# A new written-out order for the attention part of a four-layer graph-network kernel

## The chip, the core and the metric

The kernel runs on one core of one Trainium2 chip. Five engines work beside each other, each through its own list of instructions in the order in which they stand: TensorE (PE in the profile; its weight loads are PEld), VectorE (DVE), ScalarE (ACT), GpSimd (POOL) and SyncE (SP), which in this part only issues DMAs. An instruction that waits holds up everything behind it on its engine. The metric is the device time in microseconds; the median of three runs is 1857.78 us (1857.74 to 1858.48).

## The reference, cut to what matters

The input `x` is 128 batches of 64 tokens with 256 features, float32. Four layers follow, each `x = x + f(relu(layernorm(x)))`: a graph convolution with batch norms, two convolutions with four LSTMs over windows of tokens, and two attentions. Only the attentions are touched by the change:

```python
# layer 2: one head, causal, the adjacency added to the scores
q, k, v = jnp.split(h @ Wqkv, 3, axis=-1)
scores = jnp.einsum('btd,bsd->bts', q, k) / 16 + adj       # lower triangle only
x = x + (softmax(scores) @ v) @ Wo
# layer 3: four heads of 64, masked where adj == 0
q, k, v = heads(h @ W)
x = x + softmax(q @ k.T / 8 + mask) @ v
```

Here `h` is `relu(layernorm(x))` of each layer.

## The kernel before

The 8192 rows of `x` are cut into 16 chunks of 512 rows (8 batches each). Until about 1483 us of the span the first two layers run; the change leaves them alone. The attention part then takes each chunk through some 45 named steps. No scheduler decides the order: `FIRST`, `ROUND` and `LAST` (from L2234) are three strings of words such as `score2+0` (step `score2` of chunk 0), and `run` (L2270) calls the steps as they stand, `FIRST` once, `ROUND` for c = 4 to 11 with numbers relative to c, `LAST` once. A step issues its instructions on each engine that it needs, so the order of the words is the order on every engine, SP's queue of DMAs included.

Steps of layer 2, for one chunk:

- `load2` gets the chunk's normalized rows, turned to channels, from DRAM (four DMAs of 128 KB, L268). For chunks 2 to 13 they were put there during the LSTMs; chunks 14 and 15 are normalized here (`norm2`, `apply2`, `chan2`).
- `q2`, `copyq2`, `v2a`, `v2b` project queries and values for the first chunks (L1526, L1519). From chunk 4 on, seven smaller products do it: `wz`, `w5`, `w6`, `w3`, `w7`, `w4` (L1773, L1776), with `sums2` on POOL for their operands and `w11`, `w12` adding on DVE.
- `score2` (L1836) multiplies queries with keys in 64x64 pieces, `exp2`, `divide2` and `turn2` (L1668, two transposes) make the softmax, `out2` (L1867) multiplies with the values and adds to `xs`.

Steps of layer 3: `norm3` (or `norm3a`, `norm3b`) and `apply3` normalize; `square3` transposes 32x32 squares on DVE (L286) and stores to DRAM, `load3` gets the rows back as channels; `sums_h` makes operands on POOL; `qa`, `q5`, `q6`, `q3`, `qc`, `qd` (L1938) and `va`, `v5`, `v6`, `v3`, `v7`, `v4` (L2062) project, with additions `c11`, `c12`, `v11`, `v12` on DVE; `score3` (L2025), `exp3`, `sum3`, `divide3`, `turn3` and `out3` (L2142) are the attention; `keep` stores `xs` to DRAM and `back` gets it in another row order as the tile `x`; `store` adds `x` to the result (L2157) and writes it out. For chunk 15 the last steps come in two halves (`score3h`, `exp3a`, `exp3b` and so on). `res1` (three calls for each of chunks 14 and 15: transposes and store, get, add) and `pair1` (store, get) finish the LSTM layer for the last two chunks. `sums_g`, `sums_v` and `sums_w` (words for combinations of weights) run once on POOL.

`score2`, `score3`, `out2` and `out3` use PE in narrow tiles (64 rows or columns, or 32); everything else uses it whole. PSUM has eight banks, taken by the pool in order of their release; the tiles `x` and `hT3` have two buffers, `td`, `td2` and `qk` one.

Of the kernel before, what the change touches and what calls it, by code (L numbers as in the profile page):

```python
# [19 lines left out]
def kernel(  # L20
# [1440 lines left out]
    def new_hT(sc):  # L1461

        hTs[sc] = l1r.tile([P, KD, SUP * CH], F32, tag="hT", name=f"hT_{sc}")
# [99 lines left out]
    RESIDUAL_LAST = (0, 4, 5.5), (3, 5, 9)  # L1563
    FIRST = (0.5, 0.5, 1, 3, 3, 4, 4, 5, 5.5, 7, 8, 9, 10, 10), (2, 3, 4, 5, 5, 5.5, 6, 9.5, 11, 11.5, 13, 14, 15, 15.5, 17, 18, 20)
    AHEAD = (9, 10), (10, 11)
# [31 lines left out]
    with tc.manual_schedule(engines={mybir.EngineType.PE, mybir.EngineType.DVE, mybir.EngineType.Pool,  # L1597
# [4 lines left out]
        for sc in range(last + 1):  # L1602
            todo = {}

            def units(places, unit):
                for n in places:
                    todo.setdefault(n, []).append(unit)


            if sc < last:  # L1610
                for i in range(SUP):
                    units((CONV if sc else FIRST)[i], convs[(sc + 1) * SUP + i])
                new_hT(sc + 1)
# [610 lines left out]
    def store(c, t):  # L2224
# [3 lines left out]
        for r in range(2):  # L2228
# [2 lines left out]

    FIRST = """score2+0 exp2+0 divide2+0 score2+1 v2a+1 v2b+1 load2+2 res1+15 res1+14 turn2+0 exp2+1  # L2234
               res1+15 divide2+1 load2+4 v2a+2 out2+0 q2+2 norm3+0 copyq2+2 turn2+1 apply3+0 load2+3 v2b+2
               out2+1 weights3+0 score2+2 res1+14 exp2+2 norm3+1 v2a+3 q2+3 divide2+2 chan3+0 apply3+1
               res1+14 v2b+3 square3+1 turn2+2 res1+15 v3a+0 v3b+0 change+0 out2+2 sums_g+0 sums2+4 load3+1
               q30+0 k30+0 sums_v+0 norm3+2 sums_h+1 copyq2+3 q31+0 k31+0 keep+0 score2+3 apply3+2 pair1+14
               score3+0 wz+4 w5+4 sums_w+0 v5+1 exp2+3 w11+4 qa+1 q5+1 c11+1 va+1 divide2+3 exp3+0 q6+1
               square3+2 q3+1 v6+1 turn2+3 c12+1 w6+4 load2+5 v7+1 sum3+0 back+0 v3+1 qc+1 divide3+0 w7+4  # L2240
               pair1+15 load3+2 w3+4 qd+1 v11+1 turn3+0 w4+4 v4+1 sums2+5 w12+4 score3+1 pair1+14 v12+1
               pair1+15"""
    ROUND = """out3-4 store-4 sums_h-2 exp3-3 out2-1 norm3a-1 norm3b-1 score2+0 sum3-3 wz+1 w5+1 qa-2 va-2
               w6+1 load2+2 q6-2 exp2+0 q5-2 w11+1 v5-2 divide3-3 v11-2 keep-3 back-3 apply3-1 c11-2 qc-2
               w7+1 v6-2 q3-2 divide2+0 w3+1 square3-1 w4+1 w12+1 qd-2 v7-2 sums2+2 c12-2 turn3-3 load3-1
               v3-2 v4-2 v12-2 turn2+0 score3-2"""
    LAST = """out3+8 keep+9 exp3+9 out2+11 score2+12 w5+13 keep+11 norm3a+11 store+8 sums_h+10 qa+10 sum3+9
              norm3b+11 divide3+9 wz+13 q6+10 c11+10 exp2+12 w11+13 va+10 turn3+9 apply3+11 keep+10
              divide2+12 q5+10 norm2+14 w6+13 v6+10 qc+10 square3+11 w3+13 turn2+12 v5+10 v7+10 out2+12
              apply2+14 w7+13 norm3a+12 q3+10 c12+10 qd+10 norm3b+12 v4+10 v11+10 w4+13 load3+11 chan2+14  # L2250
              out3+9 w12+13 sums_h+11 apply3+12 back+10 score3+10 back+9 score2+13 qa+11 v3+10 norm2+15
              q5+11 q6+11 square3+12 v12+10 c11+11 va+11 q3+11 keep+12 sums2+14 exp3+10 v6+11 qc+11 sum3+10
              v5+11 divide3+10 wz+14 c12+11 v7+11 exp2+13 qd+11 store+9 w6+14 w11+14 v4+11 divide2+13
              score3+11 w5+14 turn2+13 load3+12 w7+14 out2+13 v3+11 w4+14 turn3+10 w3+14 apply2+15
              norm3a+13 sums_h+12 w12+14 exp3+11 norm3b+13 qa+12 score2+14 apply3+13 v11+11 v12+11 out3+10
              chan2+15 store+10 square3+13 q6+12 exp2+14 v5+12 sums2+15 divide2+14 sum3+11 va+12 q5+12
              wz+15 v11+12 load3+13 v6+12 w11+15 turn2+14 qc+12 v7+12 divide3+11 v3+12 c11+12 back+12 q3+12
              c12+12 back+11 out2+14 v12+12 w6+15 qd+12 w5+15 norm3a+14 v4+12 w7+15 sums_h+13 norm3b+14
              score3+12 turn3+11 w3+15 w4+15 apply3+14 exp3+12 qa+13 w12+15 score2+15 out3+11 exp2+15
              square3+14 keep+13 q5+13 va+13 sum3+12 divide2+15 store+11 q6+13 v5+13 q3+13 turn2+15 c11+13  # L2260
              c12+13 qc+13 out2+15 norm3a+15 v6+13 v3+13 v7+13 norm3b+15 qd+13 v4+13 load3+14 apply3+15
              divide3+12 sums_h+14 score3+13 qa+14 turn3+12 square3+15 q5+14 c11+14 exp3+13 v11+13 q6+14
              out3+12 sum3+13 back+13 load3+15 va+14 v5+14 q3+14 qc+14 v6+14 store+12 c12+14 v3+14 qd+14
              v12+13 divide3+13 score3+14 v7+14 q30+15 keep+15 v12+14 exp3+14 back+15 k30+15 q31+15 sum3+14
              k31+15 turn3+13 divide3+14 keep+14 score3h+15 exp3a+15 out3+13 sum3a+15 exp3b+15 divide3a+15
              store+13 v3a+15 v3b+15 turn3a+15 turn3+14 back+14 v11+14 v4+14 sum3b+15 out3a+15 divide3b+15
              storea+15 turn3b+15 out3+14 out3b+15 store+14 storeb+15"""
    assert (NCH, SUP) == (16, 2)

    def run(order, c):  # L2270
        for name in order.split():
            i = max(name.find("+"), name.find("-"))
            steps[name[:i]](c + int(name[i:]))

    with tc.manual_schedule(engines={mybir.EngineType.PE, mybir.EngineType.DVE,
                                     mybir.EngineType.Activation, mybir.EngineType.Pool,
                                     mybir.EngineType.SP}):
        run(FIRST, 0)
        for c in range(4, 12):
            run(ROUND, c)  # L2280
        run(LAST, 0)
    close_l2()
# [49 lines left out]
```

## Time and profile before

| | us |
|---|---|
| median of three runs | 1857.78 (1857.74 to 1858.48) |
| profiled execution, its own time | 1858.88 |
| span of its trace, first to last instruction | 1857.1 |
| first PE instruction of the attention part (`score2+0`) | 1490.76 |
| PE busy over the span | 1816.6 (98%) |
| DVE, ACT, POOL busy | 1350.6, 1058.3, 653.3 |
| issue of the last store, `storeb+15` | 1853.17 |

The profiled execution's own time is 1.8 us above its span and 1.1 us above the median. An engine's row in the timeline gives the start, the duration and, in square brackets, how long the engine had idled and what ended that; `issue` there means that the engine waited for nothing that the profile shows. PEclk is the share of the full clock that PE was granted.

### The profile page before, as it was taken

To read this page: it belongs to the slowest core of one execution; us is meant where nothing else is said; L and a number is where in the kernel's file an instruction comes from. 1 tells how busy PE (TensorE), PEld (TensorE's weight loads), DVE (VectorE), ACT (ScalarE), POOL (GpSimd) and SP (SyncE) were. 2 spreads that over 40 slices of the span, in tenths; PEclk is the share of its full clock that TensorE was granted. 3 is DMA by queue.
4 is the path that set the end of the run, shared out by engine and by line. 5 is a ranking of instruction groups with operands and counts; after the bars stand their busy time and mean duration, and the time that the engine had idled before them with its cause. 6 is when DMAs were issued, how large, how long until landed. Compare 5 with 4: busy or idle time off the path is not lost.

```text
span 1857.1 us, 41626 instructions
## 1 busy us (share of the span) xinstructions
PE 1816.6 (98%) x15847; PEld 1532.7 (83%) x15847; DVE 1350.6 (73%) x3475; ACT 1058.3 (57%) x2538; POOL 653.3 (35%) x916
## 2 busy tenths in 40 slices
PE   8999999999999999999999999999999989999997
PEld 6877866996997898799699789789979868988885
DVE  5768857667677677777877776876667667888786
ACT  5766636556557466565665655746565644445453
POOL 5865713223214323322322322332132224444432
PEclk9999999999999999999999999999999999999999
DMA  3223652133443343242353444433244145454434
GB/s 116 70 61 138 233 207 64 62 114 125 148 126 125 114 160 125 90 150 83 123 160 115 148 131 142 148 113 126 82 137 131 45 126 165 148 160 151 138 116 137
DMA packets 113417, 234.56 MB, mean 126 GB/s; under 512 B 11713, under 2 KB 77121, under 8 KB 113217
## 3 DMA queue, kind: packets, MB, share of 16 engines
q1 hardware_dynamic: 112320, 230.02, 37.8%
q8 instruction: 126, 2.06, 0.5%
q0 software_dynamic: 320, 1.05, 0.2%
q10 hardware_dynamic: 576, 0.82, 0.1%
q14 instruction: 75, 0.61, 0.1%
HBM read 164.21 MB, written 67.63 MB: 125 GB/s over the span
## 4 chain that ended last, share of the span: by engine, by line
PE 86%; DVE 6%; ACT 2%; issue 2%; POOL 2%; DMA 1%; SPq 1%; DVEq 0%; POOLq 0%; ACTq 0%
PE x L1186 22%; PE z L1186 11%; PE y L1186 6%; PE y L1133 4%; PE x L1368 4%; PE y L1368 3%; PE u L948 3%; PE v L934 3%; PE x L1133 3%; PE X L1938 2%; PE X L436 2%; PE X L512 2%; PE z L1133 2%; PE v L2062 1%; PE Y L1938 1%
## 5 line engine op out<-in xcount | busy, mean ns | idle before, releaser
L1101 ACT ACTIVATE l_gates<-l_gates,bias 128x256 f32<-128x256 f32 (+4 forms) x528 | 238.1, 498 | 211.1 <-DVE l_gates L1195 109.8
L1186 PE MATMUL x<-xd,wset 128*128 128x128 f32 (+2 forms) x1152 | 254.9, 303 | 0.8 <-ACT l_gates L1192 0.8
L1186 PE MATMUL x<-l_hd,wset 128*128 128x128 f32 (+2 forms) x1152 | 254.5, 303 | 0.0
L1252 POOL TENSOR_TENSOR l_gates<-l_gates 128x512 f32<-128x512 f32 (+2 forms) x48 | 75.3, 1569 | 368.5 <-ACT l_gates L1101 368.5
L1186 PEld LDWEIGHTS x<-xd,wset 128*128 128x128 f32 x1152 | 187.7, 191 | 6.4 <-issue 1.4
L1195 DVE TENSOR_TENSOR l_gates<-l_gates,x 128x128 f32<-128x128 f32 (+2 forms) x384 | 121.3, 322 | 97.7 <-PE x L1186 95.1
L1186 PEld LDWEIGHTS x<-l_hd,wset 128*128 128x128 f32 x1152 | 187.8, 191 | 5.0
L1195 DVE TENSOR_TENSOR l_gates<-l_gates,z 128x128 f32<-128x128 f32 (+2 forms) x384 | 102.5, 319 | 104.8 <-PE z L1186 102.8
L1186 PE MATMUL z<-l_hs,wset 128*128 128x128 f32 (+2 forms) x768 | 147.1, 304 | 0.7 <-DVE l_hs L1110 0.7
L1186 PE MATMUL z<-hT,wset 128*128 128x128 f32 (+2 forms) x768 | 146.2, 303 | 0.0
L1192 ACT COPY l_gates<-y 128x128 f32<-128x128 f32 (+2 forms) x192 | 53.2, 290 | 137.6 <-PE y L1186 131.5
L1186 PEld LDWEIGHTS z<-l_hs,wset 128*128 128x128 f32 x768 | 116.8, 191 | 5.8 <-DVE l_hs L1110 2.5
L1186 PEld LDWEIGHTS z<-hT,wset 128*128 128x128 f32 x768 | 117.1, 191 | 3.3
L1101 ACT ACTIVATE l_gates<-x,bias 128x128 f32<-128x128 f32 (+2 forms) x216 | 84.9, 393 | 28.6 <-PE x L1186 25.9
L327 POOL TENSOR_TENSOR xd<-hT 128x128 f32<-128x128 f32 (+2 forms) x72 | 42.2, 586 | 127.6 <-DVE hT L1112 113.8
L1186 PE MATMUL x<-hT,wset 128*128 128x128 f32 (+2 forms) x384 | 85.8, 305 | 0.0
L1186 PE MATMUL x<-l_hs,wset 128*128 128x128 f32 (+2 forms) x384 | 84.9, 303 | 0.0
L1186 PE MATMUL y<-l_hd,wset 128*128 128x128 f32 (+2 forms) x384 | 83.2, 309 | 0.0
L1186 PE MATMUL y<-xd,wset 128*128 128x128 f32 (+2 forms) x384 | 81.6, 304 | 0.0
L1267 ACT ACTIVATE l_gates<-l_cell 128x256 f32<-128x256 f32 (+2 forms) x144 | 55.3, 384 | 45.8 <-DVE l_cell L1266 45.2
L328 POOL TENSOR_TENSOR xd<-hT 128x128 f32<-128x128 f32 (+3 forms) x80 | 51.4, 643 | 67.0 <-DVE hT L1116 29.5
L1110 DVE TENSOR_TENSOR l_hs<-l_gates 128x256 f32<-128x256 f32 (+4 forms) x120 | 51.4, 429 | 29.5 <-ACT l_gates L1159 13.8
(408 smaller groups left out, 4695.9 us busy)
## 6 DMA issues: line engine op xcount, KB each, us to landing
wset<-wfar SPq DMA_DIRECT2D x96, 896.0 KB, 8.4
hT<-far_h SPq DMA_DIRECT2D x124, 128.0 KB, 4.2
far_h<-hm SPq DMA_DIRECT2D x16, 512.0 KB, 3.0
far_n<-xs SPq DMA_DIRECT2D x16, 512.0 KB, 3.3
xs<-far_n SPq DMA_DIRECT2D x64, 128.0 KB, 2.8
far_x<-xs SPq DMA_DIRECT2D x16, 512.0 KB, 4.2
x<-far_x SPq DMA_DIRECT2D x64, 128.0 KB, 2.7
xt<-in_x_dram SPq DMA_DIRECT2D x15, 512.0 KB, 3.9
```

The costliest lines, as they stand in the source:

```text
L328: lambda: ((third or engine).tensor_tensor(t3, b22, b12, OP.subtract), engine.tensor_tensor(t2, b22, t1, OP.subtract)),
L934: nc.tensor.matmul(banks[m], wg0_sb[:, k, m * P : (m + 1) * P], agg[:, k, :], start=(k == 0), stop=(k == KD - 1))
L948: nc.tensor.matmul(banks[j // 2][:, j % 2, :], v[:, k, j * P : (j + 1) * P], wg1_sb[:, k, :], start=(k == 0), stop=(k == KD - 1))
L1101: nc.scalar.activation(gate(q, c, part), src, AF.Tanh if q == 2 else AF.Sigmoid, bias=bs[:, q * KD + c : q * KD + c + 1])
L1133: nc.tensor.matmul(folded(self.psum(kind)), wsets[p, self.q][:, BLOCKS[kind][0], :], ox[0][kind], start=kind in (1, 5), stop=True, skip_gr ...
L1186: nc.tensor.matmul(folded(self.psum(kind)), wsets[p, self.q][:, BLOCKS[kind][i], :], (ox[self.s] if part == "x" else oh)[kind], start=firs ...
L1192: nc.scalar.copy(gate(self.q, kind // 5, halves[kind // 5]), self.psum(kind))
L1195: nc.vector.tensor_add(gate(self.q, *dst), gate(self.q, *a), self.psum(kind))
L1252: nc.gpsimd.tensor_mul(gates[:, 0, :, :n], gates[:, 0, :, :n], gates[:, 2, :, :n])
L1267: nc.scalar.activation(gate(2, c, part), cells[:, c, part], AF.Tanh)
L1368: nc.tensor.matmul(folded(ps(g, kind)), single_block(KINDS1[kind])[:, g, :], right[kind], start=kind in (2, 5, 1), stop=True, skip_group_c ...
L1938: nc.tensor.matmul(st[c, tag][:, i * CH // 2 : (i + 1) * CH // 2].rearrange("p (a n) -> p a n", n=P), w, operand3(c, kind), start=first an ...
```

## The change

Only the three strings are written anew; no step is changed. The steps in each string, with the chunks that they are called for, move between the strings: the new `FIRST` also holds `out3+0`, `store+0` and `score2+4`, and `ROUND` begins with `w3+1` instead of `out3-4`. In `FIRST` the reloads of chunks 2 and 3 (`load2`) stand ahead of that of chunk 4 with one store of `res1` between each two. In `ROUND` `out2` stands alone among full-width products, and `score2`, `score3`, `out3` follow each other. In `LAST` the ways from a store to its reload change both ways: from `keep` to `back` there are now 126, 30 and 45 steps for chunks 13, 14 and 15 (36, 12 and 3 before) but 6 and 13 for chunks 11 and 12 (124 and 62 before); from `square3` to `load3` 16 and 15 for chunks 13 and 15 (11 and 9 before), and 7, 14 and 12 for 11, 12 and 14 (16, 26 and 22 before).

```diff
-    FIRST = """score2+0 exp2+0 divide2+0 score2+1 v2a+1 v2b+1 load2+2 res1+15 res1+14 turn2+0 exp2+1
-               res1+15 divide2+1 load2+4 v2a+2 out2+0 q2+2 norm3+0 copyq2+2 turn2+1 apply3+0 load2+3 v2b+2
-               out2+1 weights3+0 score2+2 res1+14 exp2+2 norm3+1 v2a+3 q2+3 divide2+2 chan3+0 apply3+1
...
+    FIRST = """v2a+1 score2+0 load2+2 exp2+0 score2+1 res1+14 v2b+1 q2+2 exp2+1 divide2+0 turn2+0 divide2+1
+               load2+3 copyq2+2 res1+15 load2+4 v2a+2 out2+0 turn2+1 res1+15 norm3+0 v2b+2 weights3+0
+               score2+2 out2+1 q2+3 apply3+0 exp2+2 v2a+3 norm3+1 res1+14 v2b+3 copyq2+3 divide2+2 chan3+0
+               apply3+1 turn2+2 res1+15 score2+3 res1+14 v3a+0 exp2+3 v3b+0 square3+1 change+0 out2+2
+               sums_g+0 q30+0 k30+0 q31+0 sums2+4 divide2+3 turn2+3 pair1+15 norm3+2 load3+1 k31+0 sums_h+1
+               apply3+2 out2+3 score3+0 sums_w+0 norm3a+3 wz+4 keep+0 qa+1 norm3b+3 w5+4 load2+5 w6+4 q6+1
+               w3+4 pair1+15 w11+4 square3+2 sums_v+0 w12+4 back+0 q5+1 exp3+0 w7+4 keep+1 va+1 q3+1 v11+1
+               c11+1 qc+1 wz+5 c12+1 v6+1 sum3+0 divide3+0 v5+1 qd+1 pair1+14 w4+4 turn3+0 apply3+3 v7+1
+               sums2+5 score2+4 score3+1 load3+2 out3+0 pair1+14 w6+5 exp2+4 store+0 keep+2 w5+5 divide2+4
+               v4+1 qa+2"""
-    ROUND = """out3-4 store-4 sums_h-2 exp3-3 out2-1 norm3a-1 norm3b-1 score2+0 sum3-3 wz+1 w5+1 qa-2 va-2
-               w6+1 load2+2 q6-2 exp2+0 q5-2 w11+1 v5-2 divide3-3 v11-2 keep-3 back-3 apply3-1 c11-2 qc-2
-               w7+1 v6-2 q3-2 divide2+0 w3+1 square3-1 w4+1 w12+1 qd-2 v7-2 sums2+2 c12-2 turn3-3 load3-1
-               v3-2 v4-2 v12-2 turn2+0 score3-2"""
+    ROUND = """w3+1 turn2+0 keep-1 square3-1 w7+1 exp3-3 va-2 v3-3 w4+1 sums_h-2 load2+2 q6-2 c11-2 q5-2
+               w11+1 sum3-3 v6-2 w12+1 v12-3 divide3-3 load3-1 qc-2 v5-2 v11-2 out2+0 v7-2 qd-2 sums2+2
+               back-3 norm3a+0 q3-2 norm3b+0 turn3-3 c12-2 v4-2 wz+2 apply3+0 score2+1 exp2+1 score3-2
+               out3-3 store-3 divide2+1 w6+2 w5+2 qa-1"""
-    LAST = """out3+8 keep+9 exp3+9 out2+11 score2+12 w5+13 keep+11 norm3a+11 store+8 sums_h+10 qa+10 sum3+9
...
-              out3+12 sum3+13 back+13 load3+15 va+14 v5+14 q3+14 qc+14 v6+14 store+12 c12+14 v3+14 qd+14
-              v12+13 divide3+13 score3+14 v7+14 q30+15 keep+15 v12+14 exp3+14 back+15 k30+15 q31+15 sum3+14
-              k31+15 turn3+13 divide3+14 keep+14 score3h+15 exp3a+15 out3+13 sum3a+15 exp3b+15 divide3a+15
-              store+13 v3a+15 v3b+15 turn3a+15 turn3+14 back+14 v11+14 v4+14 sum3b+15 out3a+15 divide3b+15
-              storea+15 turn3b+15 out3+14 out3b+15 store+14 storeb+15"""
+    LAST = """sums_h+10 va+10 turn2+12 square3+11 exp3+9 w11+13 back+9 v3+9 v11+10 w7+13 load3+11 sum3+9
...
+              v5+13 store+11 divide3+12 turn3+12 v6+13 square3+14 divide2+15 c11+13 v12+12 turn2+15 qc+13
+              out2+15 norm3a+15 norm3b+15 v7+13 out3+12 qd+13 load3+14 v3+13 v4+13 c12+13 sums_h+14
+              apply3+15 keep+15 score3+13 va+14 qa+14 square3+15 q5+14 store+12 v11+13 q6+14 v6+14 c11+14
+              q3+14 v5+14 c12+14 exp3+13 qc+14 sum3+13 qd+14 divide3+13 load3+15 score3+14 v12+13 keep+14
+              v7+14 exp3+14 v3+14 turn3+13 q30+15 v11+14 sum3+14 k30+15 q31+15 v12+14 divide3+14 k31+15
+              turn3+14 score3h+15 out3+13 exp3a+15 sum3a+15 v3a+15 back+13 v4+14 divide3a+15 exp3b+15
+              back+15 v3b+15 turn3a+15 out3+14 store+13 sum3b+15 divide3b+15 back+14 out3a+15 storea+15
+              turn3b+15 store+14 out3b+15 storeb+15"""
```

## The prediction, made before the changed kernel ran

> **What bounds the kernel now.** First the page: one engine has no slack over the span, and the chain that ended last lies on it.
>
> ```profile
> PE 1816.6 (98%) x15847; PEld 1532.7 (83%) x15847; DVE 1350.6 (73%) x3475; ACT 1058.3 (57%) x2538; POOL 653.3 (35%) x916
> q8 instruction: 126, 2.06, 0.5%
> PE 86%; DVE 6%; ACT 2%; issue 2%; POOL 2%; DMA 1%; SPq 1%; DVEq 0%; POOLq 0%; ACTq 0%
> ```
>
> The change adds no product and removes none, so only PE's idle time, its slow time and the tail after it can move. Next the busy time by stretch: FIRST, one period of ROUND, the end.
>
> ```profile
> core 0: us, PE busy (x) PEld busy (x) DVE busy (x) ACT busy (x) POOL busy (x), PEclk, DMA share, GB/s
> 1483.00:1560.00 77.00, 71.22 (x776) 54.72 (x775) 48.79 (x122) 32.07 (x69) 27.12 (x41) 0.96 0.47 129
> 1602.00:1622.70 20.70, 20.70 (x301) 18.78 (x301) 17.30 (x38) 10.40 (x21) 9.26 (x13) 1.00 0.51 154
> 1808.00:1827.60 19.60, 17.84 (x271) 14.16 (x273) 16.35 (x33) 8.70 (x18) 6.94 (x7) 1.00 0.41 122
> 1827.60:1857.10 29.50, 19.93 (x366) 14.13 (x356) 18.36 (x33) 7.84 (x14) 3.99 (x3) 0.92 0.46 154
> ```
>
> A period is full: PE 20.7 of 20.7 us. Idle time is in FIRST and at the end. PE's timeline shows the largest piece, then a second kind of gap:
>
> ```profile
> 1506.92 1.20 PE L1836 MATMUL s<-hT,qv 128*64 128x64 f32 x32
> 1512.92 3.75 PE L1519 MATMUL v<-wg_sb,hT 128*128 128x256 f32 x8 [4.80 <-DMA hT<-far_n]
> 1516.46 4.42 PE L1526 MATMUL p_q<-hT,wg_sb 128*128 128x512 f32 x8
> ...
> 1642.67 0.92 PE L1836 MATMUL s<-hT,qv 128*64 128x64 f32 x22 [0.60 <-issue]
> ...
> 1706.27 0.62 PE L1867 MATMUL o<-qv,att 64*32 64x256 f32 x4 [1.48 <-issue]
> ...
> 1753.48 0.63 PE L1836 MATMUL s<-hT,qv 128*64 128x64 f32 x8 [2.07 <-issue]
> ```
>
> The first: `v2a+3` waits for chunk 3's reload. SP's timeline says why it is late: that reload is issued last, behind two stores that wait for DVE's transposes until 1499.85, a get and chunk 4's reload.
>
> ```profile
> 1490.42 1.74 SPq L268 DMA_DIRECT2D hT<-far_n  x4
> 1499.85 2.31 SPq L261 DMA_DIRECT2D far_h<-hm  x2
> 1503.07 1.77 SPq L268 DMA_DIRECT2D hT<-far_h  x4
> 1504.94 3.70 SPq L268 DMA_DIRECT2D hT<-far_n  x8
> ```
>
> Its price is more than 4.80: `score2+2`'s slot lasted 6.00 us instead of 1.13, and `v` then took 3.54 instead of 1.73 and `p_q` 4.25 instead of 3.46 while PEclk was 0.66 (1510 to 1520). Together 7.5.
>
> The second kind waits for no engine and always stands inside a run of narrow tiles. The trace's packets on q8 are 16384 bytes each. Counting PE's records (weight load, product and separate wait one each, two loads and two products to a float32 product, one of each to a transpose), the four stalled records, with one more at 1579.89, are 24769, 26561, 28353 and 29633: each 193 above a multiple of 256. So PE takes its program in blocks of 256 records, and one came late: the records before took 2.3 to 3.0 us, and the block was there 3.6 to 4.7 us after its predecessor began. Slots lengthened by .60, .88, 2.09 and 2.46, the last with 1.55 of slow clock after it: 7.6.
>
> **What the Trainium skill says.** "Runtime: NRT & Kernel Launch", Instruction fetch mechanics: instructions come in blocks of 16 KiB (256 instructions), fetched over the engine's own DMA queue, and the cost is mostly hidden. The trace has the same block; hidden it is not, where 256 narrow records run in under 3 us. "TensorE: Matmul & The Clock Gate", Part 1: an idle window of about 3.4 us halves the clock. The trace agrees after 4.80 us of idling, and shows it after 2.07 too. "TensorEngine Tiling (Array Packing)", Key Properties: changing the tiling mode drains the engine. Here the last full-width step before a narrow run takes 0.31 instead of 0.22 and the first after it 0.54 instead of 0.43: 0.19 a run.
>
> **The change, part by part.** I divide the time at PE's first record of `score3h+15`. Before: from 1490.76 to 1837.87, 347.1 us. Steps at their undisturbed durations (`wz` 1.75, `q5` 0.87, `v5` 0.45, `score2` 1.13, `score3` 1.02, `out3` 1.04, `out2` 1.03, `turn3` 0.88 and so on) sum to 317.7; 26 narrow runs at 0.19 give 4.9; 24.5 remain. Of these 7.5 and 7.6 are named, and 9.4 are waits in FIRST (1.1) and LAST (8.3; the longest is 1.49 at `turn3+12`, behind DVE's `divide3+12`). From `score3h+15` to the end of the span are 19.2.
>
> Work: the same, but `turn3+14` now stands before `score3h+15` (+0.9): 318.6.
>
> Reloads: `load2+3` now follows one store of `res1`. DVE reaches those four transposes after both score masks, at about 1495.9, and takes 2.0; store at 1498.0, `load2+3` issued to 1500.1, landed by 1504.3 (4.1 from issue). `q2+3`, its first reader, has 16.8 us of PE work ahead of it: 1507.6. Cover 3.3 us. Queued behind on SP: `load2+4`, both gets, `w3`'s weights (1508.6, landing 6.5 later at 1515.1; `v3a+0` wants them at 1517.1). So -7.5. Next late in FIRST is `q6+1`: `sums_w` runs on POOL behind `score3+0`'s subtraction, which waits for DVE's maximum at about 1534.0; 1.9 plus two of 0.73 give 1537.5, PE is there at 1536.65: 0.9.
>
> Narrow runs: 40 instead of 29 in all, 37 instead of 26 before `score3h+15`: 37 x 0.19 = 7.0 (+2.1).
>
> Blocks: I numbered the new order's records the same way (nine more separate waits). Two boundaries 193 above 256k now have less than 3.6 us to the next inside narrow tiles: 28 records into `score2+5` (2.4 us to the next) and 60 into `score2+10` (2.1 us). By the four measured arrivals the stalls would be 1.2 to 2.3 and 1.5 to 2.6 if triggered as there; the first begins near full-width work, where fetches started up to 2.2 us before the boundary, so I take 0.8 and 1.7: 2.5 (range 0 to 5, and 1.5 more if the clock falls). A third block starts four records ahead of a run, with the fetch begun well before: 0.
>
> ROUND's waits: laid out from PE's `w3+1` as zero, every step's inputs are ready. The shortest slack is DVE's: `score3`'s product ends at 16.3, then masks 1.33, maximum 1.13, `store` 1.2, `divide2` 1.05: 21.1; `turn2` of the next period stands at 21.6. Then `w7`'s addition (2.8) before `w4` (3.4). Behind `turn2` all of PE waits, so 0.5 is all the cover. I take 0. On SP, `load3` waits for its store (2.9 landing) with `back` queued behind; `qa` needs the tile 9.5 us later, `store` the other 7.
>
> LAST, laid out the same way from the durations of before: `turn2+15` 0.5 (`divide2+15`); `v4+13` 0.9, because `v7+13`'s addition stands on DVE behind both `norm3+15` halves; `qd+14` 0.9 for `qc+14`'s addition, and `score3+14` 0.8 for ACT's copy of `qd+14`, as `qd+14` stands just before it; 0.2 elsewhere: 3.3. Gaps under 0.6 that such a layout misses (variations of copies and DVE slowed beside POOL) came to 3.3 in the trace of before; I add 2.0. The short way of chunk 11 from `keep` to `back` sits with `load3+13` behind it; the tile lands some 2 us before `qa+13`.
>
> The tail: `score3h`, DVE's halves, `store+13`, then `back+14` into the buffer that `store+13` frees, `store+14`, `storeb+15`. DVE's and SP's order in it is the same: 19.2.
>
> Sum: 1490.8 + 318.6 + 7.0 + (0.9 + 2.5 + 3.3 + 2.0) + 19.2 = 1844.3 span. The median before stands 0.7 above the span of the profiled execution (whose own time is 1.8 above): 1845 us.
>
> **Rivals.** *Half the gain* (1849 to 1854): both block stalls at their high end with slow clock (+4), LAST as costly as before (+3.0 over my 5.3). For it: all its steps moved and each of my waits is one reading of a chain; against it: the banks and buffers that LAST's steps take are free in my layout by 0.1 us or more.
>
> *The reload's wait moves* (1854.1 to 1861, within 0.2%): the change doesn't do what it says. If chunk 3's rows land 4 us later than worked out, PE stalls again at `q2+3` and its clock falls. For it: SP still has a waiting store ahead of the reload; against it: one with four transposes, not eight, and 3.3 us of cover.
>
> *DVE's half microsecond in ROUND* (1862 to 1870): if the chain from `score3` to `divide2` runs over by more than 0.5 us, each of eight periods loses what is over, before `turn2`: 8 us for each us. To end 0.2% above the kernel before takes 16.5 us more than the forecast, 2.1 a period, so an excess of 2.6 from which it decides. For it: this is the one chain without room. Against it: DVE is 17.3 of 20.7 us busy, and its operations lasted the same in every period before.
>
> **How the numbers follow.** The forecast (1840 to 1849) has 0.68, half the gain 0.20, the moved wait 0.07, DVE 0.05. From this faster by over 0.2% has 0.88, within 0.2% (about what a measurement here can tell from no change) 0.06, slower 0.06. The range must leave out no more than 2 in 10: 1840 to 1854 holds the first two.
>
> **What would show it.** PE's wait on `hT<-far_n` at L1519 or L1526 gone, and no PEclk near 0.66 near 1515. Two `issue` gaps, inside or after `score3`/`out3` near chunk 5 and chunk 10, together 1 to 5 us. Periods of ROUND of 20.95 us, 0.19 over the undisturbed ones before. `score3h` near 1825, and the end 19.2 later. Wrong would be: a repeated wait of `tr` L1668 on DVE in ROUND, waits of PE on DMA in LAST, or a tail longer than 20.

## The result, and the profile after

The changed kernel takes 1845.45 us (median of 4 runs, 1844.12 to 1846.00) against 1858.13 us for the kernel before, run beside it: a ratio of 0.993 with a 95% interval of 0.9913 to 0.9947. The prediction was 1845.0. Its profiled execution has a span of 1842.3 us (own time 1844.12) where the one before had 1857.1.

The page after, the parts that answer to those shown before: busy time of each engine, the queue of PE's program, and the chain that ended last.

```profile
PE 1812.8 (98%) x15847; PEld 1530.5 (83%) x15847; DVE 1353.4 (73%) x3475; ACT 1061.0 (58%) x2538; POOL 656.5 (36%) x916
q8 instruction: 125, 2.05, 0.5%
PE 88%; DVE 5%; ACT 2%; POOL 2%; DMA 1%; issue 1%; SPq 0%; ACTq 0%; DVEq 0%; POOLq 0%
```

The products are the same 15847. In the chain that ended last, `issue` (time in which an engine waited for nothing that the profile names) falls from 2% to 1%, and DVE's share from 6% to 5%. Where the time lay is in the busy time by stretch:

```profile
core 0: us, PE busy (x) PEld busy (x) DVE busy (x) ACT busy (x) POOL busy (x), PEclk, DMA share, GB/s
1483.00:1560.00 77.00, 76.11 (x826) 60.58 (x825) 56.99 (x143) 38.35 (x81) 33.44 (x48) 1.00 0.55 161
1510.00:1520.00 10.00, 10.00 (x77) 8.37 (x75) 7.63 (x19) 7.11 (x15) 3.37 (x5) 1.00 0.53 135
1602.00:1622.70 20.70, 20.70 (x300) 18.71 (x299) 17.20 (x38) 10.78 (x21) 9.61 (x12) 1.00 0.51 148
1808.00:1823.00 15.00, 13.63 (x117) 8.51 (x116) 11.17 (x17) 5.55 (x10) 1.90 (x1) 1.00 0.64 187
1823.00:1842.00 19.00, 10.01 (x288) 8.36 (x285) 10.56 (x22) 4.15 (x8) 2.09 (x2) 0.85 0.35 111
```

From 1483 to 1560 PE is busy for 76.11 us of 77 (71.22 before); from 1510 to 1520 it is full at full clock. SP's timeline shows the reload of chunk 3, the first row of `hT<-far_n` here, issued between the two stores (the second is chunk 4's):

```profile
1497.74 0.34 SPq L261 DMA_DIRECT2D far_h<-hm  x1
1498.13 2.23 SPq L268 DMA_DIRECT2D hT<-far_n  x4
1503.11 0.34 SPq L261 DMA_DIRECT2D far_h<-hm  x1
1503.55 2.24 SPq L268 DMA_DIRECT2D hT<-far_n  x4
```

What PE still waits for from 1483 us to its last work, all that the chain of waits lists:

```profile
PE X L1938 <- POOL ws L1745: 0.9, 1, 0.9
PE X L1938 <- DVE qk L1985: 0.9, 1, 0.9
PE o L2142 <- DVE att L2213: 0.8, 1, 0.8
PE o L2142 <- issue: 0.7, 1, 0.7
PE tr L2208 <- DVE s L1659: 0.7, 2, 0.5
PE v L2062 <- DVE v L2075: 0.6, 1, 0.6
PE p_q L1526 <- DMA hT<-far_h: 0.4, 1, 0.4
PE tc_n L240 <- DVE o L2157: 0.4, 1, 0.4
PE tr L1668 <- DVE s L1659: 0.2, 1, 0.2
```

Columns: total us, times, longest. Together 5.6 us; the same list of the kernel before adds up to 16.5, with 4.8 for the reload and 4.5 under `issue`. The first row is `q6+1` behind `sums_w`, the second `qd+14`, the sixth `v4+13`; the third and fifth lie in the tail, and the seventh is `q30+15`, which waits for chunk 15's rows. One late block is left, in PE's timeline:

```profile
1679.29 0.21 PE L2142 MATMUL o<-v,att 64*64 64x64 f32 x1 [0.66 <-issue]
```

### The profile page after: what moved, and what is told of

It reads as the page before. It is cut to its first block, busy times and chain, and to the rows that moved or that the text cites. A ratio compares the mean times of both kernels' runs of the same rounds, so it can differ in the third digit from the quotient of the medians.

```text
span 1842.3 us, 41656 instructions
## 1 busy us (share of the span) xinstructions
PE 1812.8 (98%) x15847; PEld 1530.5 (83%) x15847; DVE 1353.4 (73%) x3475; ACT 1061.0 (58%) x2538; POOL 656.5 (36%) x916
## 4 chain that ended last, share of the span: by engine, by line
PE 88%; DVE 5%; ACT 2%; POOL 2%; DMA 1%; issue 1%; SPq 0%; ACTq 0%; DVEq 0%; POOLq 0%
PE x L1186 23%; PE z L1186 11%; PE y L1186 6%; PE y L1133 4%; PE x L1368 4%; PE y L1368 3%; PE u L948 3%; PE v L934 3%; PE x L1133 3%; PE X L1938 2%; PE X L436 2%; PE X L512 2%; PE z L1133 2%; PE v L2062 2%; PE X L1773 1%
```

## The experiments

Each kernel ran beside the kernel before on one chip; ratios are to that. "Records" are PE's weight loads, products and separate waits, counted as in the prediction; a "product" is one row of the trace, two records with its weight load.

### Chunk 3's reload alone

```
-  load2+2 res1+15 res1+14 turn2+0 exp2+1 ... apply3+0 load2+3 v2b+2
+  load2+2 res1+15 load2+3 res1+14 turn2+0 exp2+1 ... apply3+0 v2b+2
```

> The kernel before with one step moved: chunk 3's reload is issued behind the first of the two waiting stores instead of behind both stores, a get and chunk 4's reload. Theory of the prediction: the first store leaves at about 1499.9 as before, the reload's four DMAs follow by 1502 and land by 1506, before `v2a+3` asks at 1508.1. PE's wait of 4.80 us on the reload goes and with it the 1.81 and 0.79 of slow clock: 7.4 us, so 1850.6 us (1849.8 to 1851.6), PEclk 1.00 from 1510 to 1520, and the four stalls of block fetches stay where they are, 7.4 us earlier. Rival (the wait moves): PE waits again on a reload or on one of the transfers pushed back, the clock falls again, 1855 to 1858 us.

Measured: 0.9955 (0.9942 to 0.9969), 8.4 us, with an interval of 5.8 to 10.8. Its busy time by stretch:

```profile
1500.00:1510.00 10.00, 10.00 (x114) 6.35 (x99) 8.90 (x25) 3.19 (x8) 1.27 (x2) 1.00 0.93 249
1510.00:1520.00 10.00, 10.00 (x52) 7.06 (x56) 6.53 (x17) 5.91 (x13) 8.19 (x14) 1.00 0.62 146
```

No idle time, no slow clock. From `score2+0` to `score2+3` it takes 37.00 us where the kernel before took 44.41: 7.41 for an expected 7.4. The four block stalls are still there, 7.0 to 7.4 us earlier (1572.78, 1635.64, 1699.22, 1746.07), and no new wait on a reload has come. So the wait did not move. The last of the four came without slow clock after it in this execution, which is 2 us more that the reload has no part in.

### The reload put back in the changed kernel

```
-  load2+3 copyq2+2 res1+15 load2+4 v2a+2
+  copyq2+2 res1+15 load2+4 load2+3 v2a+2
```

> The changed kernel with chunk 3's reload put back behind chunk 4's, so that SP issues it behind both waiting stores. Theory: its last DMA is issued at about 1507.3 instead of 1500.4 and lands some 4.3 us later, at 1511.6, while PE asks at 1507.3 (`q2+3` is its first reader in this order): a wait of 4.3 us on the reload, and 2 to 2.6 us of slow clock after it. 6.5 us above the changed kernel (4.5 to 8), with PEclk below 0.8 from 1510 to 1520. Rival (the rest of the new order hides the reload anyway): less than 1.5 us, no slow clock.

Measured: 1852.49 us, 0.996 (0.9946 to 0.9973), 7.0 us above the changed kernel's 1845.45, which ran on another chip; by the ratios to the kernel before, 0.996 against 0.993, it is 5.6 us. PE's timeline and the stretch behind it:

```profile
1513.03 6.47 PE L1526 MATMUL p_q<-hT,wg_sb 128*128 128x512 f32 x8 [4.81 <-DMA hT<-far_n]
...
1510.00:1520.00 10.00, 6.97 (x12) 3.29 (x13) 2.13 (x9) 2.86 (x6) 1.26 (x2) 0.66 1.03 216
```

The wait is back (4.80 us in the kernel before; 4.39 to 6.13 in four more profiles with the reload in its old place), now at `q2+3`, with the clock at 0.66. `score2+3` begins 7.65 us later after `score2+0` than in the changed kernel. Of the parts of the change that ran alone this one is worth the most, and it needs none of the others.

### The same order, 96 records later

```
     keep_busy: ps = bank(...); n transposes
+    for i in range(24 if name == "a" else 0):
+        nc.tensor.matmul(ps[:64, :64], ident[:64, :64], ident[:64, :64], start=True, stop=True)
```

The added products stand 1480 us ahead of the attention, where PE waits anyway; the attention's order is that of the kernel before.

> The kernel before with 96 more records of PE's program at its very start: 24 products of 64x64 behind the first filler, in the 1.58 us in which PE waits for DVE there. The order of the attention is untouched. Theory (blocks of 256 records arrive late when a block begins 40 to 120 records inside a narrow run and ends inside it): no stall at 1579.89, 1642.67, 1706.27 and 1753.48 any more; four others, because the boundaries now fall 113 records into the run at about 1556, 84 into the one at 1618, 55 into the one at 1680 and 121 into the one at 1723, so that PE stalls (released by nothing the profile names) near 1559, 1621, 1684 and 1727, by 0.5 to 2.3 us each. Sum of the stalls about as before less a slow clock: 1853.5 to 1858.5 us. Rival (the stalls belong to the narrow tiles of these chunks, or to what the DMA queues move beside them): they stay within a few tenths of 1579.9, 1642.7, 1706.3 and 1753.5, and the time is the one before within 0.5 us.

Measured: 1.0004 (0.9996 to 1.0012). PE's timeline, the rows under `issue` (two lines of code more: L1838 is the L1836 of before, L1869 its L1867):

```profile
1563.52 0.46 PE L1838 MATMUL s<-hT,qv 128*64 128x64 f32 x8 [2.67 <-issue]
...
1628.34 0.92 PE L1838 MATMUL s<-hT,qv 128*64 128x64 f32 x22 [0.97 <-issue]
...
1691.92 0.63 PE L1869 MATMUL o<-qv,att 64*32 64x256 f32 x5 [1.46 <-issue]
...
1736.77 0.39 PE L1838 MATMUL s<-hT,qv 128*64 128x64 f32 x4 [1.58 <-issue]
```

The order's four old stalls are gone and four others stand in other chunks. They lie 4.5 to 10 us later than written down, as this execution was already 2.1 us late at the `score3` of the first of these runs (1556.84 for 1554.72; its reload wait was 6.13 instead of 4.80), and each stall pushed the next. Which record they hit does not depend on that: the boundaries expected 113, 84, 55 and 121 records into a run of 384 come round again after 256, at 369, 340, 311 and 377. That leaves 15 and 44 records, or 8 and 22 products of two records each, in `score2`; 9, or 5 products, in `out2`; and 7, or 4, in `score2`. The rows show x8, x22, x5 and x4. The places follow the count of records, and nothing else in the attention was touched.

### The changed kernel, 80 records later

The same edit with 20 products.

> The changed kernel with 80 more records of PE's program at its very start (20 products of 64x64 in the 1.58 us in which PE waits for DVE there). Theory: blocks now begin 54, 78 and 47 records into the narrow runs at about 1550, 1656 and 1719 and end inside them after 2.2, 3.0 and 2.2 us; stalls near 1552.5, 1659 and 1721.5, of 0.5 to 2.5 us each, and none at 1679. 2.5 us above the changed kernel (1 to 5). Rival (the stall at 1679 belongs to the tiles of that chunk or to its transfers): it stays, nothing new appears, the time is the same within 0.5 us.

Measured: 1846.18 us, 0.9928 (0.9916 to 0.9941): 0.7 us above the changed kernel's 1845.45 where 2.5 were expected, and by the ratios (0.9928 against 0.993) no difference. The times don't part this from the rival; the places do.

```profile
1552.64 0.34 PE L2144 MATMUL o<-v,att 64*64 64x64 f32 x5 [0.24 <-issue]
...
1721.61 0.35 PE L2144 MATMUL o<-v,att 64*64 64x64 f32 x9 [0.46 <-issue]
```

The stall at 1679 is gone, two of the three others are there, and the third block, entered at 1656.35, lasted 2.78 us and cost nothing. The places were right, the price was not: these blocks were there 2.64 and 2.87 us after their predecessors began. The packets of q8, one for each block, show the difference. In all stalls here PE goes on 2.2 to 2.9 us after the packet of the block's fetch began; but in the kernel before these fetches began 0.9 to 1.8 us after the boundary of the block ahead, in this one 0.3 to 0.5. A boundary 47 to 63 records into a run that opens with `score2` comes 0.8 to 1.1 us after the run began, since 64 of its records take 1.13 us; as many records of `score3` or `out3` take 0.5. That a boundary inside `score2` therefore finds the fetch further along fits these numbers, but is argued, not shown; why a fetch starts when it does stays open. The delay itself is no accident of one execution: in six profiles of the changed order without added records (the changed kernel twice, and with steps moved) it was 0.2 to 0.6 us at the boundary in `score2+10`, and at the one in `score2+5` the fetch began 0.4 to 1.0 us ahead and nothing stalled.

### Two narrow runs a period, alone

```
-  exp3-3 out2-1 norm3a-1 norm3b-1 score2+0 sum3-3 wz+1 w5+1
+  exp3-3 score2+0 sum3-3 wz+1 out2-1 norm3a-1 norm3b-1 w5+1
```

> The kernel before with the narrow tiles of a period of the middle part in two runs: `out2` and the two halves of `norm3` stand behind `wz` instead of ahead of `score2`. Theory: each of the eight periods pays one more change of tile size, so an undisturbed period is 20.98 instead of 20.78 us (+1.6 in all); the blocks that stalled at 1579.89 and 1642.67 now hold `wz`'s products and last 4 us, so these two stalls (0.60 and 0.88) go; those at 1706 and 1753 stay. 1.6 less 1.5 gives 1858.2 us (1857 to 1859.5): by itself the split is worth nothing here. Rival (the split is what makes the middle part faster): 1855 us or less. Rival (`out2` comes too late for the normalization and products behind it): PE waits for `apply3` or the channel sums in every period, 1862 us and more.

Measured: 0.9994 (0.9988 to 1.0001), no difference clear of noise, as expected; the first rival's 1855 us or less lies outside the interval. Undisturbed periods last 20.98 us to the hundredth. The stalls at 1579.89 and 1642.67 are gone, the two later ones stay, and a new one has come:

```profile
1556.67 0.58 PE L2142 MATMUL o<-v,att 64*64 64x64 f32 x24 [1.70 <-issue]
...
1707.04 0.45 PE L1836 MATMUL s<-hT,qv 128*64 128x64 f32 x4 [1.49 <-issue]
1753.53 0.46 PE L1836 MATMUL s<-hT,qv 128*64 128x64 f32 x8 [1.43 <-issue]
```

The new one stands at the end of a block that begins at 1549.76 in full-width work, 3.5 us ahead of the run; by the theory of the run with 96 records more it should not stall. The packet of the fetch began 4.08 us after that boundary. The stretch it fell into is full of reloads, as the DMA share (the last column but one; a packet counts whole in the stretch in which it starts, so it can pass 1) shows:

```profile
1549.00:1554.00 5.00, 5.00 (x83) 4.46 (x85) 3.25 (x6) 2.45 (x5) 1.07 (x2) 1.00 1.09 286
```

That alone does not make a fetch late. In the profile of before the same fetch began 0.84 us ahead of the boundary beside a share of 1.02, and in the two kernels that follow it began 4.02 and 3.79 us behind it and PE stalled (1.43 and 1.30); fetches as late as that also came while nothing else moved (4.10 us at a share of 0.00, in the second of the two), in blocks of mostly full-width work where nothing waited for them. So there are late blocks that the count of records does not foresee, they differ between executions, and their cause stays open.

### The last part alone, twice

The kernel before through its middle part, then the steps left over in the order of the changed kernel: first with the seam (the place where one order goes over into the other) at the end of the middle part, then with it behind `w12` of the last period, where the two orders lie a little closer: at the nearest place 6 steps have been done by only one of them, 8 in the first attempt.

> The kernel before through its middle part, and from there the remaining steps in the order of the changed kernel. Theory: nothing changes before about 1728 us (stalls at 1513, 1580, 1643 and 1706 as before). From there the stall at 1753.48 goes with its slow clock (2.46 and 1.55), since the boundary no longer falls into a narrow run; the waits of the last part fall from 8.3 us to about 3.8; three more narrow runs cost 0.6. Together 7.9 less: 1850.2 us (1848.5 to 1852). Rival (the last part's waits only change places): the stall alone is saved, 1854 to 1855.5 us.

Measured: 0.9999 (0.9991 to 1.0007), no gain for an expected 7.9 us. Part of the reason stands at the seam, in PE's timeline:

```profile
1738.83 0.41 PE L1668 MATMUL tr<-ident,s 128*128 128x128 f32 x2 [1.81 <-DVE s L1659]
```

Fifteen steps that the changed kernel has done by then come all at once here; `norm3`, `store+8` and `divide2+12` queue on DVE, and `turn2+12` waits. Behind the seam the order behaves as in the changed kernel. The expectation was also wrong in itself: it left out that `turn3+14` costs 0.9 us ahead of `score3h+15`. And part of it is this execution: from `score2+11` to `score3h+15` its profile takes 127.9 us where the kernel before took 131.1, but a late block costs 1.43 us at 1557.64 and the tail lasts 20.5 us instead of 19.2.

> The kernel before as far as `w12` of its last period, then the remaining steps in the order of the changed kernel: the last part alone, with fewer steps left over at the seam than in the attempt before. Theory: from the last period's `score2` to `score3h` of chunk 15 the kernel before takes 110.3 us and the changed one 105.0; the seam costs under 1 us. 5.2 less: 0.9972 of the kernel before (0.996 to 0.998), with the same periods of 29.37 and 19.64 us between `score2` of chunks 13, 14 and 15 as in the changed kernel. Rival (the last part saves only the stall of a late block): 0.998 to 0.999. Rival (the seam eats it, as in the attempt before): a new wait of 1.5 us or more near 1735.

Measured: 0.9978 (0.997 to 0.9986), 4.1 us. From `score2+12` to `score3h+15` it takes 104.64 us (110.26 before, 105.04 in the changed kernel), between the `score2` of chunks 13, 14 and 15 are 29.37 and 19.65, and there is no wait at the seam above 0.73. Of the 5.6 us in this stretch 4.0 are the block stall at 1753.48 with its slow clock; what is left, 1.6, is 1.2 to 1.3 against the three other profiles with the last part of before (less their block stalls). So the ratio can't rule out the rival that only the stall is saved; the stretch shows a little more than that. The seam explains about 2 us of the 4 between the two attempts (21.80 and 19.73 against 21.07 and 18.46 us between the `score2` about it), and 1.5 lie in the tail, where DVE waits 4.18 us for its last tile in the one profile and 2.71 in the other.

### A version that mends what is left

```
-  out2+3 score3+0 sums_w+0
+  out2+3 sums_w+0 score3+0
-  out2+15 norm3a+15 norm3b+15 v7+13
+  out2+15 v7+13 norm3a+15 norm3b+15
-  store+12 v11+13 ... q3+14 v5+14 c12+14 exp3+13 qc+14 sum3+13 qd+14 divide3+13 load3+15 score3+14 ... v7+14 exp3+14 v3+14
+  store+12 load3+15 v11+13 ... q3+14 c12+14 exp3+13 qc+14 v5+14 sum3+13 qd+14 v7+14 divide3+13 v3+14 score3+14 ... exp3+14
-  turn3+14 score3h+15 out3+13 exp3a+15 sum3a+15 v3a+15 back+13 ... back+15 v3b+15 turn3a+15 out3+14 store+13 ... back+14
+  score3h+15 out3+13 exp3a+15 back+13 back+15 store+13 back+14 sum3a+15 v3a+15 ... v3b+15 turn3+14 turn3a+15 out3+14
```

> The changed kernel with five of its waits taken on: `sums_w` ahead of `score3` of chunk 0 on POOL (0.9); `v7+13`'s addition ahead of both halves of `norm3+15` on DVE (0.8); `v5+14` between `qc+14` and `qd+14`, and `v7+14` and `v3+14` between `qd+14` and `score3+14` (1.0); chunk 15's reload behind `store+12` instead of two steps ahead of its reader (0.4); `turn3+14` back behind `score3h+15` (0.9). And `store+13`'s addition moved ahead of the row sums, into the 0.50 us in which DVE waits for the exponential, so that the last `x` tile is fetched 2 us earlier (from DVE's addition of `store+14`, the last to wait for it, the end follows in a fixed distance). 6 us in all if each is what ended last: 5.5 less than the changed kernel (3.5 to 6.5). Rival (each wait only uncovers the next): less than 2 us; then the same places show waits of the same size on another engine.

Measured: 1840.53 us, 0.9896 (0.9883 to 0.991), 4.9 us below the changed kernel's 1845.45 where 5.5 were expected: the sum is right within its range, its parts are not. The four edits between `out2+15` and `q30+15` gave nothing. `v4+13`'s wait is gone and `qd+14`'s halved, but `score3+13` and `turn3+13` now wait, `q30+15` waits longer for chunk 15's rows, and it starts 29.76 us after `score2+15`, as in the changed kernel to the hundredth. `q30+15` in the changed kernel, then here:

```profile
1815.37 1.95 PE L1526 MATMUL p_q<-hT,w_sb 128*128 128x512 f32 x4 [0.45 <-DMA hT<-far_h]
```

```profile
1814.44 1.95 PE L1526 MATMUL p_q<-hT,w_sb 128*128 128x512 f32 x4 [0.70 <-DMA hT<-far_h]
```

One run without those four edits, beside the mended kernel and the changed one on one chip, tests that.

> The mended kernel without its four edits in the last part (those on `v7+13`, `v5+14`, `v7+14`, `v3+14` and chunk 15's reload): only `sums_w` in the first part, `turn3+14` and `store+13` at the end. Theory after the profile of the mended kernel: `q30+15` starts 29.76 us after `score2` of chunk 15 in it and in the changed kernel alike, because chunk 15's rows come by way of `norm3`, `apply3`, `square3`, their store (4.6 us to land) and their reload; the four edits only moved PE's idle time in front of this one wait. So 29.76 us again, and a time within 0.5 us of the mended kernel's on the same chip. Rival (each edit was worth its wait): 2 us slower than the mended kernel.

> The mended kernel once more, to stand beside the run before it on one chip: 0.9896 of the kernel before (0.988 to 0.991), `q30+15` 29.76 us after `score2` of chunk 15.

> The changed kernel once more, on the same chip as the two above: 0.993 of the kernel before (0.9915 to 0.9945), 3.5 to 5 us above the mended kernel; of its block boundaries only the one 63 records into `score2+10` stalls, by 0.4 to 1.5 us.

Measured: 1840.22 us without the four edits (0.9893, 0.988 to 0.9907), 1839.65 with them (0.9891, 0.9877 to 0.9904), 1845.11 for the changed kernel (0.9919, 0.9906 to 0.9933). `q30+15` stands 29.68, 29.58 and 29.62 us after `score2+15`. The two mended versions are 0.6 us apart, well within their intervals (0.5 was expected); they beat the changed kernel by 4.9 and 5.5 us (3.5 to 5 expected), and the four edits can be left out. The 33.62 us from `score2+3` to `score2+4` become 32.46 in both (1.2 us, for 0.9 of POOL's wait). At the end, DVE's row of `store+14` in the changed kernel and then in the version with the ends alone:

```profile
1837.34 1.29 DVE L2157 TENSOR_TENSOR o<-x,o 128x512 f32<-128x512 f32 x2 [4.36 <-DMA x<-far_x]
```

```profile
1832.74 1.29 DVE L2157 TENSOR_TENSOR o<-x,o 128x512 f32<-128x512 f32 x2 [0.28 <-DMA x<-far_x]
```

The whole tail of the order hangs on that tile: `store+13` frees its buffer, `back+14` fills it, `store+14` adds to it. With `store+13`'s addition in the half microsecond in which DVE waits for the exponential, it waits 0.28 us instead of 4.36 (2.73 in the changed kernel's first profile, 2.53 in the kernel before), and from `score3h` to the end are 17.2 us instead of 20.7 (19.1), with `turn3+14` inside them.

## Why the prediction was right, and where it was off

The sum of the prediction against the same stretches of the trace, us:

| term | forecast | measured |
|---|---|---|
| narrow runs before `score3h+15`, 37 | 7.0 (0.19 each) | 7.4 (0.20 each) |
| wait on chunk 3's reload | 0 | 0 |
| `q6+1` on `sums_w` | 0.9 | 0.9 |
| late blocks | 2.5 | 0.9 |
| named waits of the last part | 3.3 | 3.4 |
| small gaps | 2.0 | 1.3 (what is left) |
| `score3h+15` starts | 1825.1 | 1823.28 |
| from there to the end | 19.2 | 19.1 |
| span | 1844.3 | 1842.3 |
| median above span | 0.7 | 3.1 |

**The reload** was right in place and size, and is shown from both sides: alone it gives 7.41 us between `score2+0` and `score2+3`, and undone it takes 7.65. The estimate of its issue (1498.0 to 1500.1) was 1498.13 to 1500.36. **The wait on POOL** came at 1537.07 for 1537.5.

**The price of a narrow run** was read from single steps; the periods show it directly: 20.78 us with one run, 20.98 with two, in the changed kernel and in the kernel before with only that edit. The prediction said 20.95; its two readings, 0.09 and 0.11 more, add up to 0.20, not to 0.19. **No engine took PE's place in the middle part**: DVE's half microsecond was enough in all eight periods, and the rival that rested on it fell. (Two small slips of addition did no harm: the durations given for DVE's chain come to 21.0, not 21.1, and those for POOL's to 1537.4, not 1537.5.)

**Late blocks** was the term that was mis-sized. Both places were right. The boundary 28 records into `score2+5` cost nothing instead of 0.8, as its fetch began 0.90 us before the boundary; that 60 records into `score2+10` (63 by the profile) cost 0.9 instead of 1.7, and 0.6 to 0.9 in the six profiles named above. The step that failed is the use of "the four measured arrivals", 3.6 to 4.7 us, for blocks that begin in `score2`, whose records are slower; there they were there after 2.64 to 2.90 us.

**The last part** was right in its sum and in two of its named waits: `v4+13` and `qd+14` cost 0.8 and 1.2 for 0.9 each; `score3+14` cost 0.4 for 0.8, `turn2+15` 0.2 for 0.5, and two of 0.4 had not been named (`chan2+15` for a bank, `q30+15` for its rows). That last one is a wait of PE on a DMA in `LAST`, which the prediction named as a sign of being wrong; at 0.4 us it left the sum standing. It is also one of the smallest in the list and the one that decides: with the larger ones mended, `q30+15` started no earlier. A wait's size in the profile is what it costs after all those before it, not what its removal gives.

**From span to median** the prediction added 0.7, by the one profiled execution of before; here it was 3.1, as the profiled execution was the fastest of the four. The 2.0 us by which the span was forecast too long and these 2.4 cancel, so the closeness of 1845.0 to 1845.45 is luck beyond about 2 us.

**Where the gain of 14.8 us between the two spans came from**, with a narrow run at 0.20 in both: the reload 7.5, blocks 6.7, waits of the first and last part 3.5, the tail 0.2; against that 2.2 for eleven more narrow runs and 0.9 for `turn3+14`. (The medians lie 12.7 apart: the two profiles are single executions.) So the reload and the blocks make up 14.2 of it, and all the rest of the new order nets 0.6. The blocks' share hangs on where their boundaries fall in these two programs. The edit to two runs a period gives no gain by itself: it pays its 1.6 us with the stalls that it removes, and how many those are depends on where the boundaries of blocks fall.

## What to carry to other kernels

Where a transfer is issued behind a waiting store on the same queue, its lateness is set by that store's data, so look at the order of the queue before the size of the transfer. Where PE is full and stalls on nothing that has a name, count its records: a block that begins and ends inside a run of tiny products can stall, at a place that can be forecast to the product and moves with any edit ahead of it; not every such block stalled here, and one stall came that the count did not foresee. Of several waits in a row, mend the one that ends last; in the last part that was the way of chunk 15's rows through memory, which `q30+15` waits for, with four PE steps between it and the largest wait shown. No run here shortened that way.

## What the runs showed of the hardware that was not expected

- The program's blocks are not always hidden. The Trainium skill ("Runtime: NRT & Kernel Launch", Instruction fetch mechanics) calls the cost of crossing a block mostly hidden; here 256 records of narrow tiles ran in 1.9 to 3.0 us, PE went on 2.2 to 2.9 us after the packet of the fetch began, and the stalls were 0.2 to 2.7 us each. The measurement decides.
- Where PE did not wait for something else, the packet of a fetch began anywhere from 2.5 us before the boundary of the block ahead to 8.5 us behind it. Those over 4 us late cost nothing where that block lasted 7.8 us or more, most of them in full-width work; two such stalled PE, by 1.43 and 1.70 us, where the block would have lasted 5.2. Much of this is fixed by the place in the program: at the boundary of record 26049 the fetch was 6.9 to 7.4 us late in each of six profiles of the changed order (the changed kernel twice, and with steps moved).
- Products that cost nothing where PE waits, 1480 us earlier, moved every block stall of the attention to another chunk: 24 of them changed four places and left the time the same (1.0004).
- PE's granted clock fell to half for 3.4 us behind block stalls of 2.07 us (kernel before) and 2.67 us (96 records later), and stayed full behind all those of 1.70 us and less. Around the reload's wait of 4.4 to 6.1 us it was half for 3.4 us in two profiles and for 6.8 in four.
- The last tile's fetch varied between executions of one kernel: DVE waited 2.73 us for it in one profile of the changed kernel and 4.36 in another.
